# The first token of three short LSTMs in seven block products instead of eight, with the schedule around it retimed

## The chip, the core and the metric

The kernel runs on one core of one Trainium2 chip, and the time is the device time of one execution in microseconds (us). Kernels are timed against each other on the same chip; the number given for a kernel is the median of its runs. One execution is recorded by the profiler; its "span" is the time from its first to its last recorded instruction, a little less than its device time. The names used below: TensorE (PE in the profile; PEld is its weight load), Vector (DVE), Scalar (ACT), GpSimd (POOL) and Sync (SP, which issues the DMAs).

## The reference, cut to what matters

The input x is 128 x 64 x 256 in float32 (batch, tokens, channels), and four layers are added to it in turn. The change lies almost wholly in the second.

```python
def layer(x, L):            # used four times
    return x + L(relu(layernorm(x)))

# layer 0: x normalised adjacency product, linear, batchnorm, relu, linear, batchnorm
# layer 1:
h = relu(einsum('ts,bsh->bth', adj, x @ Wg0 + bg0))
h = relu(einsum('ts,bsh->bth', adj, h @ Wg1 + bg1))
for p in range(1, 5):
    nw = 64 // p                                   # windows of p tokens
    wins = h[:, :nw * p, :].reshape(128 * nw, p, 256)
    last = lstm(Wih[p - 1], Whh[p - 1], bias[p - 1], wins)   # state after p steps, from zero
    h = h.at[:, arange(nw) * p + (p - 1), :].set(last)       # takes the last token's place
return h
# layer 2: attention with one head, a causal mask and an added mask, two linear maps
# layer 3: attention with four heads and a mask from adj
```

A step of an LSTM forms four gates of 256 channels, i, f, g and o, from the token and the state before; then c = sigmoid(f) c + sigmoid(i) tanh(g) and h = sigmoid(o) tanh(c). On the first step state and cell are zero, so the gate f and the products with Whh fall away: three gates, from the token alone.

## The kernel before, in words

**Tiles.** 512 columns (8 batch rows of 64 tokens) are a chunk, and there are 16 chunks. In layer 1 the channels lie on the 128 partitions in two blocks, and two chunks make a pass: a tile `hT` of 128 x 2 x 1024, eight passes in all (`sc` 0 to 7). The LSTM with p = 1 works on 1024 columns, p = 2 on 512, p = 3 on 336 and p = 4 on 256.

**Seven products.** A linear map of 256 channels to 256, with the columns cut in halves, is a 2 x 2 block product. In the usual way it takes eight products of a 128 x 128 weight block with half the columns. The kernel makes most of them in seven, after Strassen and Winograd: sums and differences of the weight blocks are made once at the start (`weight_sums`, L754 to L760, put to DRAM and read back for each p by `load_sets`, L887, as the tile `wset`), those of the operands are made as they are needed (`differences`, L313 to L316: four operations; for tokens of the input on GpSimd into the tile `xd`, for states on Vector into `hd`), and the blocks of the result are added up from the products (L1164, Vector, out of PSUM, after a copy of the first part by Scalar, L1161). The products are numbered 1 to 7: 1 takes the first channel block of the first half of the columns, 2 and 3 take the second channel block of the two halves, 5, 6, 7 and 4 take the differences. Every matmul is in float32, and a product is two matmul instructions in the profile.

**An LSTM with p > 1** (`lstm`, a generator; the numbers at its `yield`s are used below). The first token is done in the usual way: twelve products (three gates, two output blocks, two channel blocks; L1126) over all the columns, into six banks of PSUM of their own (two each of the tags `y`, `z` and `x`). Scalar makes the gates out of PSUM (L1113), Vector the cell (L1119), Scalar its tanh (L1120), Vector the state (`new_state`: L1093 inside a window, L1095 and L1099 for the last step, which goes back into `hT`) and then the differences of the state. The later steps are `Unit`s, one for each gate and step: seven kinds of product, each with a token's part and a state's part (L1155), copies (L1161), adds (L1164), gates (L1084), a GpSimd product of two gates (L1221), the cell (L1234, L1235) and its tanh (L1236). Products of the next step's token are put ahead of the state's: they need no state. The stage for p = 1 (`single`, L1340 to L1364) has seven products for each gate already. While an LSTM ends it has the operands of the next one's second token made (`ending`).

**Order.** The whole stage is written out by hand: on each engine, instructions run in the order in which the program emits them. An LSTM that stops at a `yield` lets other work in: `n` counts the `yield`s (those that yield "a" count a half), and tables say at which numbers the other generators take their next step. `single` has the places 0 to 3, p = 2 has 4 to 7, p = 3 has 8 to 13 and p = 4 has 14 to 21. The other work is: the graph convolutions of chunks of the next pass (`CONV`, `FIRST`, `BEGUN`: norm statistics, `apply`, the aggregations `agg_b` and `agg_c` of 64 short matmuls, and the 16-instruction products `v` (L915, L921) and `u` (L929, L935)); the residual of the pass before (`RESIDUAL`: transposes L1277, a way through DRAM, two adds L284 of 0.68 us); and the norm of layer 2 for chunks that are done (`AHEAD`, `LATE`, `FINAL`: through DRAM, statistics L159 and L160 on Vector, a power on GpSimd, the shift on Vector (L194), four applies on Scalar (L196), transposes). The last pass has no convolutions left; there `IDLE` puts transposes of no use on TensorE.

The middle of the function, with the first token:

```python
products = [(q, c, k) for k in range(KD) for q in GATES[:3] for c in range(KD)]
for at, (q, c, k) in enumerate(products):
    if at == 6:
        yield
    nc.tensor.matmul(banks[q, c][:, :n]..., wsets[p, q][:, 2 * k + c, :], hv[:, k, tokens 0], ...)
first_acts(0, 2); first_cell(0); first_acts(3); first_cell(1)
for c in range(KD):
    new_state(0, c, every)
```

Of the kernel before, what the change touches and what calls it, by code (L numbers as in the profile page):

```python
# [8 lines left out]
F32 = mybir.dt.float32  # L9
AF = mybir.ActivationFunctionType  # L10
# [9 lines left out]
def kernel(  # L20
# [168 lines left out]

    def apply_halves(dst, src, stats, name):  # L190

        mv, rstd = stats
        nmr = small.tile([P, NJ], F32, tag=f"ln_nmr{NJ}", name=f"nmr_{name}")
        nc.vector.scalar_tensor_tensor(nmr, mv[:, :, 0], -1.0, rstd, op0=OP.mult, op1=OP.mult)  # L194
        for j in range(NJ):
            nc.scalar.activation(dst[:, j, :], src[:, j, :], AF.Relu, bias=nmr[:, j : j + 1],  # L196
                                 scale=rstd[:, j : j + 1])
            if j % 2:
                yield
# [487 lines left out]
    with tc.manual_schedule(engines={mybir.EngineType.PE}):  # L687
# [56 lines left out]
        def weight_sums(p, q):  # L744
            w = stage.tile([P, 16, P], F32, tag="ws", name=f"ws_{p}_{q}", bufs=2)
            for i, src in enumerate((wih_t, whh_t)):
                nc.sync.dma_start(
                    w[:, 8 * i : 8 * i + 4, :].rearrange("p (k c) f -> p k (c f)", k=KD),
                    src[p - 1].rearrange("(k p) f -> p k f", p=P)[:, :, q * D : (q + 1) * D])
            yield  # L750
            v = w.rearrange("p (i b) f -> p i b f", i=2)
            for dst, a, b, op in ((4, 1, 3, OP.add), (5, 4, 0, OP.subtract), (6, 0, 1, OP.subtract),
                                  (7, 2, 5, OP.subtract)):
                nc.gpsimd.tensor_tensor(v[:, :, dst], v[:, :, a], v[:, :, b], op)  # L754
            far = dram.tile([P, 15, P], F32, tag=f"ws{p}{q}", name=f"wfar_{p}_{q}", bufs=1)
            nc.sync.dma_start(far[:, :9], w[:, :9])
            nc.sync.dma_start(far[:, 9:], w[:, 10:])
            wfar[p, q] = far
            yield
# [123 lines left out]
    def load_sets(n):  # L883
        for _ in range(min(n, len(coming))):
            p, q = coming.pop(0)
            wsets[p, q] = w1.tile([P, 15, P], F32, tag="wset", name=f"wset_{p}_{q}", bufs=6)
            nc.sync.dma_start(wsets[p, q], wfar[p, q])  # L887
# [92 lines left out]
    def convolutions(c):  # L980
# [18 lines left out]
        stats = ln_stats(xs[c], f"b{c}")  # L999
        yield  # L1000
# [23 lines left out]
    BLOCKS = {1: (0, 8), 2: (2, 9), 3: (7, 14), 4: (3, 10), 5: (4, 11), 6: (5, 12), 7: (6, 13)}  # L1024
# [14 lines left out]
    def operands_x(p, hv, name, s):  # L1039

        nw, nb, inner, tokens = columns_x(p, hv)
        m = nw * nb // 2
        t = l1.tile([P, 7 * (T // 3) * NB], F32, tag="xd", name=f"xd_{name}_{s}", bufs=2)
        t = [t[:, i * m : (i + 1) * m].rearrange("p (a b) -> p a b", b=inner) for i in range(4)]
        b = {(k, j): tokens(k, s, j) for k in range(KD) for j in range(2)}
        for f in differences(nc.gpsimd, t, b[0, 0], b[0, 1], b[1, 0], b[1, 1]):
            f()
        return {5: t[0], 6: t[1], 7: t[2], 4: t[3], 1: b[0, 0], 2: b[1, 0], 3: b[1, 1]}

    def lstm(p, hv, name, follows, x1, ending):  # L1050
# [24 lines left out]
        gates = l1.tile([P, 4, KD, CH], F32, tag="gates", name=f"gates_{name}", bufs=1)  # L1075
        cells = l1.tile([P, KD, CH], F32, tag="cell", name=f"cell_{name}", bufs=1)
        hn = l1.tile([P, KD, CH], F32, tag="hs", name=f"hs_{name}", bufs=1)
        hd = l1.tile([P, 4, CH // 2], F32, tag="hd", name=f"hd_{name}", bufs=1)
# [11 lines left out]
        def new_state(s, c, part, engine=nc.vector):  # L1090
# [6 lines left out]
            else:  # L1097
# [8 lines left out]
        ox = {1: x1}  # L1106

        banks = {(q, c): bank(f"g{q}_{name}_{c}", tag) for q, tag in ((0, "y"), (2, "z"), (3, "x"))
                 for c in range(KD)}
        def first_acts(*qs):  # L1110
            for q in qs:
                for c in range(KD):
                    nc.scalar.activation(  # L1113
                        columns_of(gate(q, c)),
                        natural(banks[q, c][:, :n].rearrange("p (w b) -> p w b", b=nb)),
                        AF.Tanh if q == 2 else AF.Sigmoid, bias=bs[:, q * KD + c : q * KD + c + 1])

        def first_cell(c):
            nc.vector.tensor_mul(cells[:, c, :n], gate(0, c), gate(2, c))  # L1119
            nc.scalar.activation(gate(2, c), cells[:, c, :n], AF.Tanh)  # L1120

        products = [(q, c, k) for k in range(KD) for q in GATES[:3] for c in range(KD)]
        for at, (q, c, k) in enumerate(products):
            if at == 6:
                yield
            nc.tensor.matmul(  # L1126
                banks[q, c][:, :n].rearrange("p (w b) -> p w b", b=nb), wsets[p, q][:, 2 * k + c, :],
                hv[:, k, : (nw - 1) * p + 1 : p, :], start=(k == 0), stop=(k == KD - 1))
        first_acts(0, 2)
        first_cell(0)  # L1130
        first_acts(3)
        first_cell(1)
        for c in range(KD):
            new_state(0, c, every)
            if not c:
                dh[0]()
# [67 lines left out]
        each(A, pe(5, "x"), pe(3, "x"), pe(2, "x"))  # L1204
        yield
        for s in range(1, p):
# [4 lines left out]
            each(A, pe(5, "h"), do("copy", 5), pe(1), do("copy", 1), pe(3, "h"), pe(2, "h"), pe(6), do("u4"),  # L1211
# [88 lines left out]
    def block_sums(b, name):  # L1300

        t = []
        for i in range(2):
            part = l1.tile([P, 7 * (T // 3) * NB], F32, tag="xd", name=f"xd_{name}_{i}", bufs=2)
            for a in range(0, 2 * CH, CH):
                v = part[:, a : a + CH]
# [7 lines left out]
    def single(b, name, t, ending):  # L1314
# [5 lines left out]
        gates = l1.tile([P, 4, KD, CH], F32, tag="gates", name=f"gates_{name}", bufs=1)  # L1320
        cells = l1.tile([P, KD, CH], F32, tag="cell", name=f"cell_{name}", bufs=1)
        more = l1.tile([P, KD, CH], F32, tag="hs", name=f"hs_{name}", bufs=1)
# [90 lines left out]
    operands = {}  # L1413

    def lstms(sc, hT):
# [4 lines left out]
        def ending(p):  # L1420

            if p < SKIP:
                operands[p + 1] = operands_x(p + 1, hv, names[p + 1], 1)
# [40 lines left out]
    def ahead(c):  # L1464

        yield from to_pairs(c)
        stats = ln_stats(xs[c], f"n2_{c}")
        yield
# [16 lines left out]
    RESIDUAL = (0, 3, 4), (2, 5, 5.5)  # L1485
    CONV = (3, 4, 4, 5, 5.5, 7, 8, 9, 10, 10), (3, 4, 4, 11, 11.5, 13, 14, 15, 15.5, 17, 18, 20)
    BEGUN = (11, 11, 13, 14, 16), (17, 17.5, 21)
    FIRST = (1, 2, 3, 3, 4, 4, 5, 5.5, 7, 8, 9, 10, 10), (1, 2, 4, 5, 6, 8, 11, 11.5, 13, 14, 15, 15.5, 17, 18, 20)
    AHEAD = (4, 5, 7, 12, 14, 19), (6, 7)
    LATE = 5, 6, 8, 9  # L1490
    IDLE = {5: 4, 7: 18, 9: 10, 13: 14, 15: 8}
    FINAL = (4, 5, 9.5, 10, 12, 13), (6, 7, 11.5, 14, 14, 15)
# [25 lines left out]
    with tc.manual_schedule(engines={mybir.EngineType.PE, mybir.EngineType.DVE, mybir.EngineType.Pool,  # L1518
                                     mybir.EngineType.Activation, mybir.EngineType.SP}):
        last = NCH // SUP - 1  # L1520
        for sc in range(last + 1):
# [7 lines left out]
            if sc > 1:  # L1529
                units(LATE[:1], aheads[sc * SUP - 3])  # L1530
# [9 lines left out]
            if sc > 1:  # L1540
                units(LATE[1:], aheads[sc * SUP - 3])
# [548 lines left out]
```

## Time and profile before

| | us |
|---|---|
| median of 7 runs | 1868.53 |
| fastest and slowest of them | 1867.3, 1869.97 |
| the profiled execution | 1869.97 |
| its span | 1868.2 |
| first-token products L1126 in it, the first and the last start | 294.3, 1456.2 |
| first-token products L1126 in it, 576 instructions | 185.8 |
| later products L1155 in it, the largest group (1152 instructions) | 255.7 |
| residual adds L284 from `hT`, 32 | 0.68 each |

The profile gives busy time of each engine, a timeline of instructions (start, duration, line, operation, output tile <- input tiles, shape, count, and in brackets how long the engine was idle before it and what ended that), groups of like instructions (count, busy time, mean in ns, idle time before them), the chain of work that ended last in order of time, and the waits of an engine by what it waited for. Matmuls overlap a little in the records, so the busy time of a group is larger than the time that it takes of TensorE; the steps of the chain do not overlap.

### The profile page before, as it was taken

The numbers are of one execution on the slowest core, as the hardware profiler recorded it, in microseconds if no ns is written. First come the engines' busy times: TensorE is split into PE (matmuls) and PEld (weight loads), VectorE is DVE, ScalarE is ACT, GpSimd is POOL, SyncE is SP. The second block draws the span as 40 slices with busy tenths as digits, with TensorE's granted clock in tenths as the row PEclk, the third lists the DMA queues.
The fourth block names the chain that finished last, engine by engine and source line by source line (L and its number), as shares of the span: only waits on it lengthen the run. The fifth ranks groups of instructions, "written<-read, shape, count | busy, mean of one in ns | idle before, by whom it ended". The sixth has DMA issues, their size and how long they took to land.

```text
span 1868.2 us, 39078 instructions
## 1 busy us (share of the span) xinstructions
PE 1846.0 (99%) x15077; PEld 1477.1 (79%) x15077; DVE 1250.8 (67%) x3150; ACT 1013.4 (54%) x2284; POOL 554.0 (30%) x704
## 2 busy tenths in 40 slices
PE   8999989999999999999999999999999999999998
PEld 6877855996897799699589689878969967777776
DVE  5767856567467666667766766766566567776776
ACT  5766635556456455655654655655565534444453
POOL 5865712123122222212322311222132114322232
PEclk9999999999999999999999999999999999999999
DMA  3223651235333533333433443343144244544433
GB/s 115 69 65 140 236 207 57 96 123 169 111 119 141 164 131 131 109 114 121 160 119 120 164 146 126 142 125 124 61 142 149 71 158 136 151 145 144 141 114 114
DMA packets 111273, 241.45 MB, mean 129 GB/s; under 512 B 11504, under 2 KB 74864, under 8 KB 111088
## 3 DMA queue, kind: packets, MB, share of 16 engines
q1 hardware_dynamic: 110192, 237.09, 37.8%
q8 instruction: 119, 1.95, 0.4%
q0 software_dynamic: 320, 1.05, 0.2%
q10 hardware_dynamic: 576, 0.82, 0.1%
q14 instruction: 66, 0.54, 0.1%
HBM read 170.50 MB, written 68.42 MB: 128 GB/s over the span
## 4 chain that ended last, share of the span: by engine, by line
PE 90%; DVE 5%; ACT 2%; issue 1%; POOL 1%; DMA 1%; SPq 0%; DVEq 0%; ACTq 0%; POOLq 0%
PE x L1155 22%; PE z L1155 11%; PE g L1126 9%; PE y L1155 6%; PE v L1580 5%; PE x L1340 4%; PE y L1340 3%; PE u L929 3%; PE v L915 3%; PE p_q L1587 3%; PE X L1776 3%; PE X L423 2%; PE X L499 2%; PE Y L423 1%; PE Y L1776 1%
## 5 line engine op out<-in xcount | busy, mean ns | idle before, releaser
L1155 PE MATMUL x<-xd,wset 128*128 128x128 f32 (+2 forms) x1152 | 255.7, 304 | 1.4 <-DVE gates L1164 1.4
L1155 PE MATMUL x<-hd,wset 128*128 128x128 f32 (+2 forms) x1152 | 254.7, 303 | 0.0
L1221 POOL TENSOR_TENSOR gates<-gates 128x512 f32<-128x512 f32 (+2 forms) x48 | 75.1, 1565 | 498.7 <-ACT gates L1084 498.7
L1164 DVE TENSOR_TENSOR gates<-gates,x 128x128 f32<-128x128 f32 (+2 forms) x384 | 120.7, 320 | 151.3 <-PE x L1155 148.3
L1084 ACT ACTIVATE gates<-gates,bias 128x256 f32<-128x256 f32 (+4 forms) x384 | 172.6, 489 | 90.3 <-DVE gates L1164 90.3
L1164 DVE TENSOR_TENSOR gates<-gates,z 128x128 f32<-128x128 f32 (+2 forms) x384 | 102.2, 317 | 146.3 <-PE z L1155 146.3
L1155 PEld LDWEIGHTS x<-xd,wset 128*128 128x128 f32 x1152 | 187.8, 191 | 7.5 <-DVE gates L1164 2.5
L1155 PEld LDWEIGHTS x<-hd,wset 128*128 128x128 f32 x1152 | 187.8, 191 | 4.9
L1126 PE MATMUL g<-hT,wset 128*128 128x256 f32 (+2 forms) x576 | 185.8, 477 | 0.1
L1126 PEld LDWEIGHTS g<-hT,wset 128*128 128x128 f32 x576 | 109.4, 191 | 69.1 <-issue 39.1
L1161 ACT COPY gates<-y 128x128 f32<-128x128 f32 (+2 forms) x192 | 54.0, 292 | 198.0 <-PE y L1155 196.0
L1155 PE MATMUL z<-hs,wset 128*128 128x128 f32 (+2 forms) x768 | 146.6, 303 | 0.2 <-DVE hs L1093 0.2
L1155 PE MATMUL z<-hT,wset 128*128 128x128 f32 (+2 forms) x768 | 146.5, 303 | 0.0
L1155 PEld LDWEIGHTS z<-hs,wset 128*128 128x128 f32 x768 | 117.2, 191 | 3.9 <-DVE hs L1093 0.6
L1155 PEld LDWEIGHTS z<-hT,wset 128*128 128x128 f32 x768 | 117.2, 191 | 3.4
L1113 ACT ACTIVATE gates<-g,bias 128x512 f32<-128x512 f32 (+2 forms) x144 | 75.2, 559 | 42.3 <-PE g L1126 41.7
L1084 ACT ACTIVATE gates<-x,bias 128x128 f32<-128x128 f32 (+2 forms) x192 | 74.8, 390 | 29.7 <-PE x L1155 26.5
L1155 PE MATMUL x<-hT,wset 128*128 128x128 f32 (+2 forms) x384 | 86.0, 306 | 0.0
L1155 PE MATMUL x<-hs,wset 128*128 128x128 f32 (+2 forms) x384 | 84.9, 303 | 0.0
L1236 ACT ACTIVATE gates<-cell 128x256 f32<-128x256 f32 (+2 forms) x144 | 55.2, 383 | 47.3 <-DVE cell L1235 47.3
L1155 PE MATMUL y<-hd,wset 128*128 128x128 f32 (+2 forms) x384 | 79.4, 309 | 0.0
L1595 POOL TENSOR_TENSOR s<-s,mx 128x256 f32<-128x256 f32 (+2 forms) x33 | 40.4, 1225 | 128.0 <-DVE mx L1594 120.2
(326 smaller groups left out, 4169.5 us busy)
## 6 DMA issues: line engine op xcount, KB each, us to landing
wset<-wfar SPq DMA_DIRECT2D x96, 960.0 KB, 6.6
hT<-far_h SPq DMA_DIRECT2D x124, 128.0 KB, 3.2
far_h<-hm SPq DMA_DIRECT2D x16, 512.0 KB, 2.8
far_n<-xs SPq DMA_DIRECT2D x16, 512.0 KB, 3.4
xs<-far_n SPq DMA_DIRECT2D x64, 128.0 KB, 4.6
far_x<-xs SPq DMA_DIRECT2D x16, 512.0 KB, 3.0
x<-far_x SPq DMA_DIRECT2D x64, 128.0 KB, 3.2
xt<-in_x_dram SPq DMA_DIRECT2D x15, 512.0 KB, 4.1
```

What stands on the lines that cost most here:

```text
L423: nc.tensor.matmul(self.banks[tag][:, i * CH // 2 : (i + 1) * CH // 2], w, self.at[kind], start=first and not i, stop=True, skip_group_che ...
L915: nc.tensor.matmul(banks[m], wg0_sb[:, k, m * P : (m + 1) * P], agg[:, k, :], start=(k == 0), stop=(k == KD - 1))
L929: nc.tensor.matmul(banks[j // 2][:, j % 2, :], v[:, k, j * P : (j + 1) * P], wg1_sb[:, k, :], start=(k == 0), stop=(k == KD - 1))
L1084: nc.scalar.activation(gate(q, c, part), src, AF.Tanh if q == 2 else AF.Sigmoid, bias=bs[:, q * KD + c : q * KD + c + 1])
L1113: nc.scalar.activation(columns_of(gate(q, c)), natural(banks[q, c][:, :n].rearrange("p (w b) -> p w b", b=nb)), AF.Tanh if q == 2 else AF. ...
L1126: nc.tensor.matmul(banks[q, c][:, :n].rearrange("p (w b) -> p w b", b=nb), wsets[p, q][:, 2 * k + c, :], hv[:, k, : (nw - 1) * p + 1 : p, ...
L1155: nc.tensor.matmul(folded(self.psum(kind)), wsets[p, self.q][:, BLOCKS[kind][i], :], (ox[self.s] if part == "x" else oh)[kind], start=firs ...
L1164: nc.vector.tensor_add(gate(self.q, *dst), gate(self.q, *a), self.psum(kind))
L1221: nc.gpsimd.tensor_mul(gates[:, 0, :, :n], gates[:, 0, :, :n], gates[:, 2, :, :n])
L1340: nc.tensor.matmul(folded(ps(g, kind)), wih1[:, g, KINDS1[kind], :], right[kind], start=kind in (2, 5, 1), stop=True, skip_group_check=True)
L1580: nc.tensor.matmul(ps[:, i, :], hT[:, k, j, :], w[:, k, first : first + D], start=(k == 0), stop=(k == KD - 1))
L1776: nc.tensor.matmul(st[c, tag][:, i * CH // 2 : (i + 1) * CH // 2].rearrange("p (a n) -> p a n", n=P), w, st[c, "o7"][kind], start=first an ...
```

## The change

Five things are changed together.

1. The first token of p = 2, 3 and 4 is done in seven products for each gate, by a new class `First`: 21 products of half the columns (L1127 after the change), Scalar's copies of two of them (L1131), Vector's adds (L1134: twelve), gates by `act` (L1095) out of the sums, and for one quarter out of PSUM. The gates 0 and 2 use one bank each of the tags `y` and `z`, gate 3 two of the tag `x`; so the products 1, 6, 7 and 4 of a gate follow each other in one bank. There is one more `yield`, of "a", after the first half of the state. The later products, adds and gates are L1180, L1189 and L1095 there, the cells L1152, L1159, L1259 and L1260, the states L1104, L1106 and L1110, the differences L327 to L330.
2. The plain weight blocks that only the twelve products used leave the sets, which have 14 blocks in place of 15 and are put to DRAM by three DMAs in place of two. The differences of the first token are made on GpSimd like the second's, and the tile `xd` has three buffers in place of two. Of the second token's products ahead of the state, number 5 is moved to its place beside the state's part.
3. The tiles `gates`, `cell`, `hs` and `hd` are made once for the stage in place of once for each LSTM.
4. The statistics of a norm are done in two steps of two tiles each, and the shift (minus mean over deviation) by two operations on GpSimd in place of one on Vector.
5. The tables are new. `agg_b` of the next pass's first chunk, which stood between the twelve products of p = 2, is at place 3, ahead of them; the residual add of the second chunk is at 8.5 in place of 5.5; the norm of layer 2 begins in one pass and ends in the next for both chunks.

```diff
+    def norm_halves(src, name):
...
+        for j in range(NJ):
+            nc.vector.bn_stats(st[:, j, :], src[:, j, :])
+            nc.vector.bn_aggr(mv[:, j, :], st[:, j, :])
+            if j == NJ // 2 - 1:
+                yield
...
+        rsqrt(rstd, mv[:, :, 1], EPS)
+        nc.gpsimd.tensor_tensor(nmr, mv[:, :, 0], rstd, OP.mult)
+        nc.gpsimd.tensor_scalar(nmr, nmr, -1.0, None, op0=OP.mult)
+        yield rstd, nmr
...
-            wsets[p, q] = w1.tile([P, 15, P], F32, tag="wset", name=f"wset_{p}_{q}", bufs=6)
+            wsets[p, q] = w1.tile([P, 14, P], F32, tag="wset", name=f"wset_{p}_{q}", bufs=6)
...
-        t = l1.tile([P, 7 * (T // 3) * NB], F32, tag="xd", name=f"xd_{name}_{s}", bufs=2)
+        t = l1.tile([P, 2 * CH], F32, tag="xd", name=f"xd_{name}_{s}", bufs=3)
...
-        gates = l1.tile([P, 4, KD, CH], F32, tag="gates", name=f"gates_{name}", bufs=1)
-        cells = l1.tile([P, KD, CH], F32, tag="cell", name=f"cell_{name}", bufs=1)
-        hn = l1.tile([P, KD, CH], F32, tag="hs", name=f"hs_{name}", bufs=1)
-        hd = l1.tile([P, 4, CH // 2], F32, tag="hd", name=f"hd_{name}", bufs=1)
+        gates, cells, hn, hd = lstm_tiles
...
+        class First:
+
+            def __init__(self, q, tags):
+                self.q, self.ps = q, [bank(f"{t}{q}_{name}_{i}", t) for i, t in enumerate(tags)]
+
+            def psum(self, kind):
+                return self.ps[kind in (5, 3)][:, m:n] if kind in (2, 3) else self.ps[kind in (5, 3)][:, :m]
+
+            def product(self, kind):
+                nc.tensor.matmul(folded(self.psum(kind)), wsets[p, self.q][:, BLOCKS[kind][0], :], ox[0][kind],
+                                 start=kind in (1, 5), stop=True, skip_group_check=True)
...
+        firsts = [First(q, tags) for q, tags in ((0, "yz"), (2, "yz"), (3, "xx"))]
+
+        def all_first(*fs):
+            for f in fs:
+                for u in firsts:
+                    f(u)
...
+        all_first(made(1), lambda u: u.copy(0, 0, 1), made(5), lambda u: u.copy(1, 1, 5))
+        yield
+        all_first(made(2), lambda u: u.add((0, 0), (0, 0), 2), made(3), made(6), lambda u: u.add((0, 1), (1, 1), 6),
+                  made(7), lambda u: u.add((1, 1), (1, 1), 7), lambda u: u.add((0, 1), (0, 1), 3), made(4),
+                  lambda u: act(u.q, 0, every, gate(u.q, 0)))
+        nc.vector.tensor_mul(cells[:, 0, :n], gate(0, 0), gate(2, 0))
+        nc.scalar.activation(gate(2, 0), cells[:, 0, :n], AF.Tanh)
+        all_first(lambda u: act(u.q, 1, halves[0], u.psum(4)),
+                  lambda u: act(u.q, 1, halves[1], gate(u.q, 1, halves[1])))
+        new_state(0, 0, every)
+        dh[0]()
+        yield "a"
...
-        each(A, pe(5, "x"), pe(3, "x"), pe(2, "x"))
+        each(A, pe(3, "x"), pe(2, "x"))
...
-            each(A, pe(5, "h"), do("copy", 5), pe(1), do("copy", 1), pe(3, "h"), pe(2, "h"), pe(6), do("u4"),
+            each(A, pe(5, "h" if s > 1 else "xh"), do("copy", 5), pe(1), do("copy", 1), pe(3, "h"), pe(2, "h"), pe(6), do("u4"),
...
-                operands[p + 1] = operands_x(p + 1, hv, names[p + 1], 1)
+                operands[p + 1] = {s: operands_x(p + 1, hv, names[p + 1], s) for s in range(2)}
...
-    RESIDUAL = (0, 3, 4), (2, 5, 5.5)
-    CONV = (3, 4, 4, 5, 5.5, 7, 8, 9, 10, 10), (3, 4, 4, 11, 11.5, 13, 14, 15, 15.5, 17, 18, 20)
-    BEGUN = (11, 11, 13, 14, 16), (17, 17.5, 21)
-    FIRST = (1, 2, 3, 3, 4, 4, 5, 5.5, 7, 8, 9, 10, 10), (1, 2, 4, 5, 6, 8, 11, 11.5, 13, 14, 15, 15.5, 17, 18, 20)
-    AHEAD = (4, 5, 7, 12, 14, 19), (6, 7)
-    LATE = 5, 6, 8, 9
+    RESIDUAL = (0, 3, 5.5), (2, 5, 8.5)
+    CONV = (3, 4, 5, 5.5, 7, 8, 9, 10, 10), (5, 5, 6, 9.5, 11, 11.5, 13, 14, 15, 15.5, 17, 18, 20)
+    BEGUN = (11, 11, 14.5, 17, 17, 20, 21), (17.5, 19, 21)
+    FIRST = (1, 1, 1, 2, 3, 4, 4, 5, 5.5, 7, 8, 9, 10, 10), (1, 2, 4.5, 5, 5, 6, 9.5, 11, 11.5, 13, 14, 15, 15.5, 17, 18, 20)
+    AHEAD = (6, 7), (9, 10)
+    LATE = (4.5, 4.5, 5.5, 9, 19.5), (9, 9.5, 11, 12, 21)
+    LATEST = (4.5, 4.5, 5.5, 9, 9.5), (9.5, 9.5, 10, 11, 11.5)
     IDLE = {5: 4, 7: 18, 9: 10, 13: 14, 15: 8}
-    FINAL = (4, 5, 9.5, 10, 12, 13), (6, 7, 11.5, 14, 14, 15)
+    FINAL = (6, 7, 11, 11, 12, 15, 15.5), (9, 10, 13, 13, 16, 17, 17.5)
...
-            if sc > 1:
-                units(LATE[:1], aheads[sc * SUP - 3])
...
             if sc > 1:
-                units(LATE[1:], aheads[sc * SUP - 3])
+                for i in range(SUP):
+                    units((LATEST if sc == last else LATE)[i], aheads[(sc - 2) * SUP + i])
```

## The prediction, made before the changed kernel was run

> **What bounds the kernel now.** I read the page's first part, then the busy time by stage, then what TensorE waited for while the LSTMs run, then the timeline around the places that the diff touches.
>
> ```profile
> span 1868.2 us, 39078 instructions
> ...
> PE 1846.0 (99%) x15077; PEld 1477.1 (79%) x15077; DVE 1250.8 (67%) x3150; ACT 1013.4 (54%) x2284; POOL 554.0 (30%) x704
> ```
>
> Busy time by stage; this is one pass over two chunks in the LSTM stage (TensorE, weight loads, Vector, Scalar, GpSimd, granted clock, DMA):
>
> ```profile
> 580.00:726.00 146.00, 145.77 (x1027) 118.42 (x1026) 97.54 (x257) 82.21 (x197) 37.06 (x44) 1.00 0.38 132
> ```
>
> TensorE's waits between 290 and 1470 us are only these:
>
> ```profile
> PE x L1155 <- DVE gates L1164: 1.4, 6, 0.2
> PE agg_b L214 <- ACT cv L196: 1.2, 1, 1.2
> PE y L1155 <- ACT gates L1113: 0.7, 1, 0.7
> ```
>
> So TensorE is the limit: 3.3 us of waiting in 1180, at full clock. Products taken away are time saved, one for one; every wait that the change brings is time lost, one for one.
>
> **The products: 20.0 us saved.** The chain in order of time has the first tokens of p = 3 and p = 4, and fillers of known size:
>
> ```profile
> 490.91 3.45 PE u L929 x16
> 494.37 6.78 PE g L1126 x24
> 502.86 1.09 PE agg_c L214 x64
> ...
> 539.08 5.18 PE g L1126 x24
> 545.60 3.46 PE u L929 x16
> ```
>
> A product is two instructions. 24 instructions of 336 columns take 6.78 us, of 256 columns 5.18; of 512 columns twice 5.15 (605.23, x12). Together 22.26 a pass. After, each has 21 products of half the width. One of 256 columns is 3.46/8 = 0.4325 us, one of 168 is 0.285 (steps 506.83, 507.12, 507.40), one of 128 is 0.2235 (551.12 to 551.34). 21 x (0.4325 + 0.285 + 0.2235) = 9.08 + 5.99 + 4.69 = 19.76. Saved 2.50 a pass, 20.0 over eight.
>
> **The waits inside the 21 products.** The old order ran twelve products into six banks with no reader between. The new one reuses a bank: 7 needs Vector's add of 6, 4 needs the add of 7, and only two other products stand between. The turnaround:
>
> ```profile
> 507.12 0.45 PE L1155 MATMUL x<-hd,wset 128*128 128x168 f32 x2
> 507.40 0.45 PE L1155 MATMUL x<-xd,wset 128*128 128x168 f32 x2
> 507.67 0.33 DVE L1164 TENSOR_TENSOR gates<-gates,x 128x168 f32<-128x168 f32 x1 [3.49 <-PE x L1155]
> ```
>
> The product's slot ends at 507.40, the add starts 0.27 later and takes 0.33; Vector to TensorE is 0.05 (an add of 560.57 ends, the product starts at 560.90). p = 3: 0.65 against two slots of 0.57, twice 0.07, 0.15 in all. p = 4: 0.27 + 0.28 + 0.05 = 0.60 against 0.447, twice, 0.31. p = 2: 0.74 against 0.865, nothing. Eight passes: 2.5 us for p = 4; p = 3's 0.15 is in the next part.
>
> **The wait for token 0's state, p = 3.** Before, Scalar's gates began when 7 of 12 products were done. Now every gate waits for adds at the end, and the products that need the state come after four x products and the filler. Counted from the first of the 21: the sixes' first ends at 3.71, the products at 6.13; Vector's last-but-three adds end at 5.80 and the first add of 3 at 6.05 (0.33 alone, 0.245 back to back: two took 0.57 at 531.19). Then Scalar:
>
> ```profile
> L1084 ACT ACTIVATE gates<-gates,bias 128x336 f32<-128x336 f32 x64 | 34.8, 570 | 24.5 <-DVE gates L1164 24.5
> ```
>
> 0.57, 0.46 for each one behind it: two done at 7.10; cell product 0.51, 7.65; tanh 0.48, 8.15; state 0.51 and its difference 0.33, 9.05. TensorE stands at 6.13 + 1.14 (four x) + 1.09 (agg) + 0.285 = 8.65 and gets the operand at 9.10: 0.45 lost. For the second channel block Scalar does three gates from PSUM (0.40, then 0.30) and two of 0.42 and 0.33 by 9.75, but Vector's queue has two residual adds between (moved to 8.5 of the schedule; L284 from hT, 20.5 us for 32, 1.28 a pair): 10.35. Product, tanh, state (0.51 + 0.48 + 0.51): 11.93. TensorE has seven more products of cover, until 11.10: 0.83 lost. Last, two chunk applies of 0.54 stand on Scalar ahead of the copies that free the banks for 6: about 0.2. Sum 0.15 + 0.45 + 0.83 + 0.2 = 1.65 in passes 2 to 7; pass 1 has no apply (1.43), pass 0 no residual add either (1.0). Total 12.3 us. At p = 4 the filler is u (3.46): operand at 7.6, wanted at 9.4. At p = 2 it is v (3.43): 12.7 against 14.7, the second block 17.0 against 17.7 with four statistics of 0.53 in Vector's queue. No cost there; without that cover it would be 1 to 2 us each.
>
> **The start of p = 2.** Products 1 and 5 use channel block 0, product 2 the last state of the single-step stage:
>
> ```profile
> 605.07 4.46 PE L1126 MATMUL g<-hT,wset 128*128 128x512 f32 x10
> ...
> 607.95 1.20 DVE L1356 TENSOR_TENSOR hT<-cell,gates 128x512 f32<-128x512 f32 x1 [0.16 <-ACT gates L1353]
> ```
>
> It lands at 609.15, 4.1 us after that stage's last product. Before, 5.15 us of products and agg_b covered it. After, agg_b (1.1, moved ahead) and six products (2.6) give 3.7: 0.44 lost with the hand-over, in six passes, 2.6 us. In passes 3 to 6 four transposes (1.42 at 1418.99), placed at 21, go ahead of the single stage's adds. Part of the delay is absorbed; I take 0.55 each, 2.2 us, between 0 and 1.4.
>
> **The last pass** has no convolutions, only idle transposes whose number is unchanged:
>
> ```profile
> 1372.29 10.46 PE L1126 MATMUL g<-hT,wset 128*128 128x512 f32 x24
> ...
> 1376.03 1.19 DVE L1356 TENSOR_TENSOR hT<-cell,gates 128x512 f32<-128x512 f32 x1 [0.17 <-ACT gates L1353]
> ```
>
> The state lands 4.9 us after 1372.3, cover is 2.6: 2.3 lost. At p = 2 the state of token 0 then comes 1.05 and 1.2 late (0.45 of filler in place of 3.43). At p = 3 the state lands 2.66 after the first product, against 1.71: 0.95. At p = 4, 0.74, and the statistics of chunk 13 (2.1 us) stand ahead of the first adds, 1.0 more; then 0.6 and 0.4 as above with 0.9 of filler. Sum 8.2, of which 0.7 was there before (the third wait above): 7.5.
>
> **Parts that I cost at nothing.** The weight set is one block of fifteen smaller (960 KB, 6.6 us to land, no TensorE wait on a DMA in the stage); the far copy takes three issues in place of two, twelve more on SP while Seven2 runs, where SP is ahead. If it were not, one landing of 2.8 us each way bounds it. Norm shifts: Vector loses an operation of about 0.15 us, GpSimd gains 0.20 + 0.24 (L356, L357) behind a power of 1.04. The reader is Scalar's apply, and of TensorE's waits only agg_b's 1.2 us comes from an apply: between -0.3 and +0.4 us a chunk, 0 taken. One tile for the stage drops waits like Scalar's at 590.81 on GpSimd's state; TensorE waited for none of them, 0, at best -0.8 a pass. Block operands of token 0: four more GpSimd operations, 24 times (0.54 at 168); in p = 3 done 2.4 us after the start, wanted at 3.4; late by the whole 1 us only if GpSimd is held by other work.
>
> A row on that: the state of 607.95 took 1.20 us beside GpSimd's L315, the same line 0.69 at 607.09. The Trainium skill, page "SBUF — State Buffer", section "SBUF: two separate sides", says that Vector with two SBUF inputs and GpSimd take one shared port by an exclusive lock for a whole instruction. By that rule the new block adds (one input in PSUM) would be untouched and the sum stands as it is; if every start lost the 0.5 us of that row, it would be 24 x 0.5 = 12 us worse.
>
> **Sum.** -20.0 + 2.5 + 12.3 + 2.6 + 2.2 + 7.5 = +7.1 us. The profiled execution took 1869.97 us (span 1868.2 and 1.8 around it), 1.4 over the median of 1868.53. So 1877 for it, **1875.5** for the median; I say 1875. Each wait is a difference of long chains, good to perhaps 0.3 us, and the same one repeats in seven or eight passes.
>
> **Rivals.** (1) **Token 0's state is back in time.** One place: p = 3, Scalar's gates. It decides if the operand is there 8.65 us after the first product instead of 9.10, and the second by 11.1 instead of 11.9, as when Scalar's gates go out faster than 0.46 apiece or the residual add slips into a gap. Then the 12.3 shrinks to 0.15 x 8 = 1.2 and the last pass, having the same chain, to about half, 3.7: -20.0 + 2.5 + 1.2 + 2.6 + 2.2 + 3.7 = -7.8, 1860.5. For it: Vector is 67% and Scalar 54% busy. Against: they are idle because they wait in this very chain. (2) **Waits and saving cancel**, the sum lying 4 to 10 us lower than mine: 1868.5. For it: all the waits are computed, none seen. (3) **Queues run into each other**: Vector gets 12 more adds a start and the waits above feed the next ones, with 0.5 us (1.20 against 0.69 at 607) for each of 24 starts: +7.1 + 12 = 1887.5. Against: three adds take 0.82 us at p = 3 and three products 0.855. (4) That the change does not do what it says: the instruction order of the changed kernel shows 21 half products at each of 24 starts, so no chance of its own.
>
> **How the numbers follow.** Forecast 0.46, rival 1 0.27, rival 2 0.19, rival 3 0.08. A measurement tells 0.2% (3.7 us) from no change: faster 0.27, same 0.19, slower 0.54. From 1858 to 1885: from rival 1's time less 2.5 (the bounds of the small parts) to most of the way to rival 3; its far end and a full saving are left out. The forecast's own range is 1872 to 1883.
>
> **What would show it.** L1126 is replaced by L1127 with 504 products, TensorE busy down by about 20 us, idle up by 27. Waits of L1180 on hd and hs (L327, L1104) near 0.45 and 0.8 at each p = 3, waits of L1127 on Vector near 0.15 at p = 4, waits of L1127 on hT (L1378) of 0.4 and, in the last pass, above 2. If p = 3's waits are absent, rival 1 holds. I would be wrong by more if TensorE's busy time did not fall by 20 us, or waits came on GpSimd's xd.

## The result, and the profile after

The changed kernel takes **1873.48 us** (median of 13 runs, 1872.77 to 1874.33), the kernel before 1868.04 on the same chip (33 runs, 1867.3 to 1869.97). The ratio is 1.0028 with a 95% interval of 1.0021 to 1.0036: 5.4 us slower, where 7 were forecast.

The first part of the page, after:

```profile
span 1870.9 us, 40786 instructions
...
PE 1838.8 (98%) x15509; PEld 1513.5 (81%) x15509; DVE 1321.7 (71%) x3410; ACT 1051.3 (56%) x2500; POOL 613.4 (33%) x856
```

TensorE's busy time fell by 7.2 us, not by 20. That isn't a smaller saving: the records of a product's two matmuls run 0.45 us where its slot (the time from its start to the next one's in an unbroken row) is 0.285, so a wait of up to 0.16 us shows as busy time. The waits that are long enough to show, between 285 and 1470 us (waited-for line: total, times, longest):

```profile
PE z L1180 <- DVE l_hs L1104: 3.7, 8, 0.8
PE x L1362 <- DVE l_gates L1386: 2.3, 1, 2.3
PE y L1127 <- DVE hT L1378: 2.2, 7, 1.1
PE x L1127 <- ACT l_gates L1367: 1.0, 1, 1.0
PE y L1127 <- ACT l_gates L1131: 0.9, 2, 0.6
PE y L1127 <- POOL xd L328: 0.7, 1, 0.7
PE y L1180 <- ACT l_gates L1095: 0.6, 1, 0.6
```

They add up to 11.4 us (two more, of 0.3 and 0.2, are left out here), where before there were 3.3. To see the short ones too, take the time from the start of each matmul to the start of the next, less the usual slot of its shape: in the LSTM stage that excess is about 35 us before (some 20 of it at the short agg matmuls) and about 58 after, 23 more, against 20 saved. The table below says the same: its three longest stretches (pass 0, passes 1 to 6, last pass) are 3.1 us longer in all, with 20.0 us of products less. The lengths of the stretches, from the starts of their first matmuls; the third column belongs to the first experiment, the last pass is taken to the first matmul of layer 2:

| us | before | after | twelve_all |
|---|---|---|---|
| pass 0 | 158.92 | 158.02 | 156.90 |
| pass 3, p = 1 and p = 2 | 60.68 | 60.17 | 60.96 |
| pass 3, p = 3 | 44.71 | 45.19 | 44.71 |
| pass 3, p = 4 | 48.12 | 47.61 | 47.56 |
| passes 1 to 6 | 920.74 | 917.52 | 919.09 |
| last pass | 143.16 | 150.38 | 142.05 |

So the loss is not spread: seven passes are 4.1 us shorter, the last is 7.2 longer. The rest of the program differs by less than 1 us on either side. (The two profiled executions, 1869.97 and 1872.77 us, are the slowest of the first and the fastest of the second, so the traces can place 2.8 of the 5.4 us.)

### The profile page after: what moved, and what is told of

It reads as the page before. It is cut to its first block, busy times and chain, and to the rows that moved or that the text cites. A ratio compares the mean times of both kernels' runs of the same rounds, so it can differ in the third digit from the quotient of the medians.

```text
span 1870.9 us, 40786 instructions
## 1 busy us (share of the span) xinstructions
PE 1838.8 (98%) x15509; PEld 1513.5 (81%) x15509; DVE 1321.7 (71%) x3410; ACT 1051.3 (56%) x2500; POOL 613.4 (33%) x856
## 4 chain that ended last, share of the span: by engine, by line
PE 83%; DVE 9%; ACT 4%; POOL 2%; issue 1%; DMA 1%; SPq 0%; DVEq 0%; ACTq 0%; POOLq 0%
PE x L1180 22%; PE z L1180 11%; PE y L1180 5%; PE v L1605 5%; PE y L1127 4%; PE u L943 3%; PE v L929 3%; PE p_q L1612 3%; PE y L1362 3%; PE X L1801 3%; PE x L1362 3%; PE x L1127 2%; PE X L437 2%; PE X L513 2%; PE z L1127 1%
## 5 line engine op out<-in xcount | busy, mean ns | idle before, releaser
L1095 ACT ACTIVATE l_gates<-l_gates,bias 128x256 f32<-128x256 f32 (+4 forms) x528 | 238.1, 498 | 211.9 <-DVE l_gates L1189 110.0
L1180 PE MATMUL x<-xd,wset 128*128 128x128 f32 (+2 forms) x1152 | 255.1, 303 | 0.2 <-ACT l_gates L1186 0.2
L1180 PE MATMUL x<-l_hd,wset 128*128 128x128 f32 (+2 forms) x1152 | 254.6, 303 | 0.0
L1189 DVE TENSOR_TENSOR l_gates<-l_gates,z 128x128 f32<-128x128 f32 (+2 forms) x384 | 102.3, 317 | 130.6 <-PE z L1180 128.6
L1180 PEld LDWEIGHTS x<-xd,wset 128*128 128x128 f32 x1152 | 187.8, 191 | 5.8 <-issue 0.5
L1180 PEld LDWEIGHTS x<-l_hd,wset 128*128 128x128 f32 x1152 | 187.9, 191 | 4.9
L1189 DVE TENSOR_TENSOR l_gates<-l_gates,x 128x128 f32<-128x128 f32 (+2 forms) x384 | 121.1, 321 | 92.2 <-PE x L1180 88.4
L1180 PE MATMUL z<-l_hs,wset 128*128 128x128 f32 (+2 forms) x768 | 147.3, 304 | 3.7 <-DVE l_hs L1104 3.7
L1180 PE MATMUL z<-hT,wset 128*128 128x128 f32 (+2 forms) x768 | 146.2, 303 | 0.0
L1180 PEld LDWEIGHTS z<-l_hs,wset 128*128 128x128 f32 x768 | 116.8, 191 | 9.4 <-DVE l_hs L1104 6.1
L1180 PEld LDWEIGHTS z<-hT,wset 128*128 128x128 f32 x768 | 117.2, 191 | 3.3
L1095 ACT ACTIVATE l_gates<-x,bias 128x128 f32<-128x128 f32 (+2 forms) x216 | 84.7, 392 | 30.8 <-PE x L1180 28.1
L1180 PE MATMUL x<-hT,wset 128*128 128x128 f32 (+2 forms) x384 | 85.9, 305 | 0.0
L1180 PE MATMUL x<-l_hs,wset 128*128 128x128 f32 (+2 forms) x384 | 84.9, 303 | 0.0
L327 POOL TENSOR_TENSOR xd<-hT 128x128 f32<-128x128 f32 (+2 forms) x72 | 42.5, 590 | 128.2 <-DVE hT L1106 100.0
L1180 PE MATMUL y<-l_hd,wset 128*128 128x128 f32 (+2 forms) x384 | 83.6, 310 | 0.3 <-DVE l_hd L327 0.2
L1180 PE MATMUL y<-xd,wset 128*128 128x128 f32 (+2 forms) x384 | 81.9, 305 | 0.9 <-ACT l_gates L1095 0.6
```

The costliest lines, as they stand in the source:

```text
L1095: nc.scalar.activation(gate(q, c, part), src, AF.Tanh if q == 2 else AF.Sigmoid, bias=bs[:, q * KD + c : q * KD + c + 1])
L1180: nc.tensor.matmul(folded(self.psum(kind)), wsets[p, self.q][:, BLOCKS[kind][i], :], (ox[self.s] if part == "x" else oh)[kind], start=firs ...
L1189: nc.vector.tensor_add(gate(self.q, *dst), gate(self.q, *a), self.psum(kind))
```

## The experiments

**1. Twelve products again, the rest as changed** (`twelve_all`). The old block with its yield "a" after the first half of the state, sets of 15 blocks, two `xd` buffers, and no differences of the first token on GpSimd.

```diff
-        all_first(made(1), lambda u: u.copy(0, 0, 1), made(5), lambda u: u.copy(1, 1, 5))
...
+        products = [(q, c, k) for k in range(KD) for q in GATES[:3] for c in range(KD)]
+        for at, (q, c, k) in enumerate(products):
...
```

> The changed kernel with the first token of every LSTM back in twelve full products (15-block weight sets and two xd buffers, as before the change, since both do not fit beside each other); its tables, the norm's two halves, the shifts on GpSimd and the single set of tiles stay. Theory 1 (all of the +5.4 us is the seven products' own balance: 20.0 us of TensorE saved, 23 us of new waits in the LSTM stage): 1868 to 1870, waits of the stage back near 36 us by the starts of the matmuls, of which agg steps are some 20. Theory 2 (the products gain, and the retimed tables and moved norm operations cost more than that): clearly above 1873.5, up to 1890 if the whole 20 us were won net.

Measured 1865.84 (0.9988, 0.9979 to 0.9997): a little faster than before. TensorE waits in the stage, between 290 and 1470 us:

```profile
PE x L1401 <- DVE l_gates L1425: 2.3, 1, 2.3
PE z L1219 <- DVE l_hs L1108: 0.2, 1, 0.2
```

Theory 1 holds in its cause, but the time lies 2.2 us below its range: seven products cost 7.6 us against this kernel, and the other parts of the change win 2.4 against the kernel before. (The wait of 2.3 us stands in both lists, so it is not the seven products'.) Against it, the seven products change passes 0 to 6 by -0.45 us in all (saving and waits cancel almost exactly) and the last pass by +8.3.

**2. Twelve products in the last pass alone** (`twelve_last`).

```diff
+        if old_first(p, name):      # sc == 7
+            products = [(q, c, k) for k in range(KD) for q in GATES[:3] for c in range(KD)]
...
+        else:
             all_first(made(1), lambda u: u.copy(0, 0, 1), made(5), lambda u: u.copy(1, 1, 5))
```

> The changed kernel with twelve full products in the last pass alone, seven in passes 0 to 6. Theory 1 (the last pass, without convolutions to lie between, lost 7.2 us from its start to the start of layer 2, and passes 0 to 6 won 4.1): the last pass falls from 150.4 to about 143 to 145 us, total 1866 to 1868, below the kernel before. Theory 2 (the last pass loses by its new tables, not by the seven products): the last pass stays at 148 to 150 us, total 1872 to 1873.5.

Measured 1869.34 (1.0003, 0.9994 to 1.0012). The last pass fell to 142.05, so its loss is the seven products', not the new tables'. But the total stayed above theory 1's 1866 to 1868: p = 3 had grown from 45.19 to 45.82 us in passes 1 to 6. The kernel differs there only in the weight sets and in two `xd` buffers for three, which the next one separates.

**3. Two xd buffers, nothing else** (`xd_two_buffers`).

```diff
-        t = l1.tile([P, 2 * CH], F32, tag="xd", name=f"xd_{name}_{s}", bufs=3)
+        t = l1.tile([P, 2 * CH], F32, tag="xd", name=f"xd_{name}_{s}", bufs=2)
```

> The changed kernel with two xd buffers in place of three, nothing else. Theory 1 (what kept twelve_last at 1869.3 in place of 1866 is the missing third buffer: GpSimd waits 1.49 us for the old one and then runs beside Vector's cell and state of p = 3, which take 0.80 and 0.83 us in place of 0.51): p = 3 grows from 45.19 to 45.8 us in passes 1 to 6, total 1877 to 1878. Rival (it was the 15-block set): 1873.5.

The tile is made at two places, and both have the edit. Measured 1879.0 (1.0059, 1.0045 to 1.0073), p = 3 at 45.81: the buffer. The time lies 1 us above theory 1's range; the last pass grew too, by 0.8 us. In p = 3 of pass 3, first GpSimd, then Vector:

```profile
807.00 0.54 POOL L327 TENSOR_TENSOR xd<-hT 128x168 f32<-128x168 f32 x1 [1.49 <-PE x L1127]
807.50 0.54 POOL L328 TENSOR_TENSOR xd<-hT 128x168 f32<-128x168 f32 x1
807.99 0.81 POOL L329 TENSOR_TENSOR xd<-hT,xd 128x168 f32<-128x168 f32 x1
```

```profile
807.59 0.81 DVE L1152 TENSOR_TENSOR l_cell<-l_gates 128x336 f32<-128x336 f32 x1 [0.63 <-ACT l_gates L1095]
808.95 0.83 DVE L1104 TENSOR_TENSOR l_hs<-l_gates 128x336 f32<-128x336 f32 x1 [0.55 <-ACT l_gates L1153]
```

The late GpSimd operations are not waited for. They harm by running beside Vector's cell and state, which then take 0.81 and 0.83 us in place of 0.51, in the chain that TensorE waits for: 0.62 us together, as much as p = 3 grew.

**4. The residual add of the second chunk half a place later** (`residual_9`).

```diff
-    RESIDUAL = (0, 3, 5.5), (2, 5, 8.5)
+    RESIDUAL = (0, 3, 5.5), (2, 5, 9)
```

> The changed kernel with the residual add of the second chunk at place 9 in place of 8.5, so behind the second half of p = 3's first state on Vector. Theory 1 (the two adds of 1.28 us stand ahead of the second cell product, which waits for Scalar's gates only until 0.5 us earlier): the wait of z on the state in p = 3, 0.59 us net in passes 1 to 6, falls to about 0.1, total -3 us, 1870.5. Rival (Scalar's order, six gates and a tanh, holds the second half anyway): wait unchanged, 1873.5.

Measured 1873.46 (1.0026, 1.0016 to 1.0036). Neither theory as written: the wait on the state went in passes 1 to 6, and no time was won. In p = 3 of pass 3, Vector and then TensorE:

```profile
809.74 1.28 DVE L298 TENSOR_TENSOR xs<-xs,hT 128x512 f32<-128x512 f32 x2
...
812.03 0.55 DVE L1189 TENSOR_TENSOR l_gates<-l_gates,x 128x168 f32<-128x168 f32 x2
```

```profile
808.90 1.41 PE L1180 MATMUL z<-l_hs,wset 128*128 128x168 f32 x8
...
812.39 0.55 PE L1180 MATMUL x<-xd,wset 128*128 128x168 f32 x2 [0.37 <-DVE l_gates L1189]
```

The two adds now stand, with two statistics behind them, ahead of the block adds of the next step, and TensorE waits there: p = 3 takes 45.36 us in passes 2 to 6, where it took 45.19. From 808.34 to 813 Vector has no gap in this trace; a move inside such a stretch only names another wait. (In pass 1, which has no such statistics, the same move won 0.47 us.)

**5. and 6. The small parts undone** (`undo_small`: the shift on Vector and new tiles for each LSTM; `shift_vector`: the shift alone).

```diff
-        nc.gpsimd.tensor_tensor(nmr, mv[:, :, 0], rstd, OP.mult)
-        nc.gpsimd.tensor_scalar(nmr, nmr, -1.0, None, op0=OP.mult)
+        nc.vector.scalar_tensor_tensor(nmr, mv[:, :, 0], -1.0, rstd, op0=OP.mult, op1=OP.mult)
         yield rstd, nmr
...
-        gates, cells, hn, hd = lstm_tiles
+        gates, cells, hn, hd = new_tiles()      # undo_small alone
```

> The changed kernel with the norm's shift back on Vector in one operation, and the four tiles made anew for each LSTM; seven products, tables and the two halves of the statistics stay. Theory 1 (these parts cost and bring nothing, as the prediction took them): 1873.5, within 1.5. Rival (one of them is part of the loss, or hides a gain): 2 us or more away on either side.

> The changed kernel with only the norm's shift back on Vector; the single set of tiles stays. Theory 1 (in undo_small, 35 us slower, the whole loss is that Scalar's first copy must wait until the last reader of the old tiles is done, Vector's state of the LSTM before; the trace shows that copy idle 1.39 us for it): 1873.5, within 1.5. Rival (the shift in one Vector operation delays applies and with them the chain): between 1880 and 1908.

Measured 1908.65 (1.0213, 1.0199 to 1.0227) and 1904.77 (1.0194, 1.018 to 1.0208). I had put the 35 us down to the tiles; it was the shift, and the tiles are left with 3.9. The second time lies in the rival's range, but no wait of TensorE on an apply came with it; what came was in Vector's queue. Vector in `shift_vector`:

```profile
DVE nmr_n L202 <- POOL rstd_n L100: 21.4, 14, 2.4
DVE nmr_b L202 <- POOL rstd_b L100: 20.5, 14, 1.5
```

An operation of 0.16 us stands directly behind GpSimd's power and holds Vector's whole queue, 41.9 us in 28 waits. TensorE then waits 14.8 us for block adds and 8.5 for states in that trace.

**7. The shift on Vector, one yield later** (`shift_vector_late`), as before the change.

```diff
     def apply_halves(dst, src, stats, name):
+        nc.vector.scalar_tensor_tensor(nmr, mv[:, :, 0], -1.0, rstd, op0=OP.mult, op1=OP.mult)
```

> The changed kernel with the shift back on Vector where it was before the change: with the applies, one yield after the power on GpSimd, not directly behind it as in shift_vector. Theory 1 (the 31 us of shift_vector come from Vector's queue standing 1.3 to 2.4 us for GpSimd's power, 28 times and more, not from the operation): 1873.5 to 1875. Rival (the operation on Vector costs wherever it stands): above 1885.

Measured 1878.37 (1.0052, 1.0037 to 1.0067): 4.9 over the changed kernel, beyond what theory 1 allowed, far below the rival. The place is worth 26 us, the operation itself 5; its trace is 2.1 us longer than the changed kernel's in pass 0, 1.6 in passes 1 to 6 and 1.8 in the last pass. Why the operation costs as much there was not followed further.

**8. New tiles with twelve products** (`twelve_own_tiles`): `twelve_all` with the `new_tiles()` of the diff above.

> Twelve full products everywhere as in twelve_all, and the four tiles made anew for each LSTM. Theory 1 (a new set of tiles costs only where a writer comes early, and with twelve products Scalar's first gate comes seven products after the start): 1866, within 1.5. Rival (the new tiles cost in any case): far above, near 1900.

Measured 1867.08 (0.9992, 0.9982 to 1.0001); every section is as long as in `twelve_all` within 0.15 us. As theory 1 has it: new tiles cost nothing clear here, where the first writer comes late, and about 4 us with `First`, whose copies write them early. (In `undo_small` TensorE waits 6.0 us in 9 places for those copies, in `shift_vector` 0.6 in 2.)

**9. to 12. Seven products where they pay.** `seven_p2_steady` has them for p = 2 in passes 1 to 6 and twelve products elsewhere. The others try to remove its wait at the start of p = 2: `seven_p2_early_hm` moves four transposes, `seven_p2_swap` puts product 3 ahead of 2, `seven_p2_after_state` forms GpSimd's differences in another order.

```diff
+        return int(p > 2 or sc in (0, 7))      # old_first, in all four
...
-    RESIDUAL = (0, 3, 5.5), (2, 5, 8.5)        # seven_p2_early_hm
+    RESIDUAL = (0, 3, 5.5), (1, 5, 8.5)
...
-            all_first(made(2), lambda u: u.add((0, 0), (0, 0), 2), made(3), made(6), ...    # seven_p2_swap
+            all_first(made(3), made(2), lambda u: u.add((0, 0), (0, 0), 2), made(6), ...
...
-        for f in differences(nc.gpsimd, t, b[0, 0], b[0, 1], b[1, 0], b[1, 1]):    # seven_p2_after_state
-            f()
+        if p == 2 and s == 0:
+            t1, t2, t3, t4 = t
+            for dst, x, y, op in ((t1, b[0, 1], b[0, 0], OP.subtract), (t4, b[1, 0], b[1, 1], OP.subtract),
+                                  (t2, b[1, 1], t1, OP.subtract), (t3, b[1, 1], b[0, 1], OP.subtract),
+                                  (t4, t4, t1, OP.add)):
+                nc.gpsimd.tensor_tensor(dst, x, y, op)
+        else:                                  # the four differences as before
...
```

> Seven products only for p = 2 in passes 1 to 6, twelve everywhere else. From the section lengths of the profiles: p = 1 and p = 2 together take 60.67 to 60.97 us a pass with twelve and 59.86 to 60.17 with seven, p = 3 44.71 against 45.19, p = 4 47.56 against 47.60. Theory 1 (the sections add up, each pays by itself): 1865.8 - 6 x 0.8 = 1861, below both kernels. Rival (what p = 2 wins is lost in the next section's waits): 1865 to 1866.

> As seven_p2_steady, with the four transposes of the second chunk's residual (2.1 us on Vector) at place 1 in place of 2, so not directly ahead of the last gates of p = 1. Theory 1 (they make the state late that the first products 2 of p = 2 wait for, 0.43 net a pass): that wait falls to 0 to 0.1, 1858.5. Rival (on Vector they only push the earlier adds of p = 1, and TensorE waits there instead): no gain, 1861, or a loss of up to 1 us a pass.

> As seven_p2_steady, with product 3 ahead of product 2. Product 3 needs the half of the last state of p = 1 that Vector writes first, product 2 the half that it writes last. Theory 1 (the wait at the start of p = 2, 0.43 net a pass, is for that last half alone, and three products of 0.43 more cover it): the wait goes, 1862.2 - 6 x 0.43 = 1859.7. Rival (the adds of 2 then come later and something behind them waits): 1862.

> As seven_p2_steady, with GpSimd's differences for the first token of p = 2 formed in another order, with one operation more (first the difference of the two states of channel block 1, which waits for the last state, then the others), so that GpSimd starts after Vector's last state of p = 1 and not beside it. Theory 1 (that state takes 1.20 us in place of 0.69 because GpSimd works beside it): it takes 0.69, lands 0.5 us earlier, the wait at the start of p = 2 (0.43 net a pass) goes, 1862.2 - 6 x 0.43 = 1859.7. Rival (the 1.20 has another cause, as its layout): it stays 1.20 and the time 1862.2; or the later differences make product 6 wait: above 1862.2.

| kernel | us | ratio to before, interval | p = 2, pass 3 |
|---|---|---|---|
| seven_p2_steady | 1862.24 | 0.9964, 0.9952 to 0.9977 | 40.66 |
| seven_p2_early_hm | 1869.44 | 1.0004, 0.9995 to 1.0013 | 40.96 |
| seven_p2_swap | 1865.02 | 0.9983, 0.9974 to 0.9992 | 41.11 |
| seven_p2_after_state | 1859.18 | 0.9952, 0.9938 to 0.9965 | 40.28 |

The first is nearest to theory 1 (1861): the sections add up, to 1 us. The second is its rival, and worse: p = 1 grew from 19.52 to 20.81 us, because TensorE now waits for block adds behind the moved transposes. The third is a miss of both: product 3, which goes into the same bank as product 5, had to wait for Scalar's copies of 5, and these for the last state of p = 1, which still reads the part of `l_gates` that they write:

```profile
PE z L1131 <- ACT l_gates L1135: 3.3, 6, 0.6
```

The same state was waited for, by another way. The fourth is theory 1. GpSimd and Vector in `seven_p2_steady`:

```profile
757.42 0.73 POOL L328 TENSOR_TENSOR xd<-hT 128x256 f32<-128x256 f32 x1 [2.69 <-DVE hT L1417]
758.11 1.18 POOL L329 TENSOR_TENSOR xd<-hT,xd 128x256 f32<-128x256 f32 x1
```

```profile
757.51 1.20 DVE L1417 TENSOR_TENSOR hT<-l_cell,l_gates 128x512 f32<-128x512 f32 x1 [0.17 <-ACT l_gates L1414]
```

and in `seven_p2_after_state`:

```profile
756.55 0.74 POOL L1069 TENSOR_TENSOR xd<-hT 128x256 f32<-128x256 f32 x1 [3.55 <-DVE hT L1424]
```

```profile
755.77 0.69 DVE L1424 TENSOR_TENSOR hT<-l_cell,l_gates 128x512 f32<-128x512 f32 x1 [0.17 <-ACT l_gates L1421]
```

With one GpSimd operation more, but none beside it, the state takes 0.69 us and the wait is gone. This kernel is 9 us faster than before and 14 faster than the change.

## Why the prediction was right

**The sign and the size held, and so did the main reason**: 20 us of products saved, a little more than that in new waits. Term by term, against the kernel before unless said otherwise:

- **The saving.** In p = 3 of pass 3 the 21 products take 6.36 us with 0.37 of waiting, 5.99 without: as computed.
- **Inside the 21 products, p = 4: 0.31 forecast, 0.53 measured.** The turn between two trios was sized well: the first product of the next trio comes 0.17 and 0.19 late, near the 0.15 of the sum. What the sum left out is that a product behind a wait takes longer itself, here by 0.10 and 0.07 us (its two matmuls start 0.21 and 0.19 us apart in place of 0.11, at 845.89 and 846.85). The row before the change from which the hand-over was read has it too: 0.49 us for the two matmuls at 560.90, in place of 0.39. At p = 3 the same turns 0.15 into 0.37 (0.09 and 0.11 late, 0.10 and 0.08 longer). Against `twelve_all`, p = 4 wins nothing (47.61 and 47.56).
- **p = 3: 1.65 forecast, 1.28 measured** (net of what was there). This is the chain that carried the forecast; Scalar, Vector and TensorE after the change, from the first of the 21 at 797.18:

```profile
803.31 1.50 ACT L1095 ACTIVATE l_gates<-l_gates,bias 128x336 f32<-128x336 f32 x3 [3.92 <-DVE l_gates L1134]
```

```profile
804.38 0.51 DVE L1152 TENSOR_TENSOR l_cell<-l_gates 128x336 f32<-128x336 f32 x1 [0.63 <-ACT l_gates L1095]
805.44 0.51 DVE L1104 TENSOR_TENSOR l_hs<-l_gates 128x336 f32<-128x336 f32 x1 [0.55 <-ACT l_gates L1153]
805.98 0.33 DVE L327 TENSOR_TENSOR l_hd<-l_hs 128x168 f32<-128x168 f32 x1
806.23 1.28 DVE L298 TENSOR_TENSOR xs<-xs,hT 128x512 f32<-128x512 f32 x2
807.44 0.50 DVE L1159 TENSOR_TENSOR l_cell<-l_gates 128x336 f32<-128x336 f32 x1
808.48 0.51 DVE L1104 TENSOR_TENSOR l_hs<-l_gates 128x336 f32<-128x336 f32 x1 [0.55 <-ACT l_gates L1160]
```

```profile
806.37 0.55 PE L1180 MATMUL y<-l_hd,wset 128*128 128x168 f32 x2
...
809.05 1.41 PE L1180 MATMUL z<-l_hs,wset 128*128 128x168 f32 x8 [0.42 <-DVE l_hs L1104]
```

The gates start at 6.13 (forecast 6.05 plus the hand-over), the difference is done at 9.13 (9.05), the second state at 11.81 (11.93). The chain was right within about 0.1 us; TensorE stood elsewhere. It lost 0.37 inside the 21 products (forecast 0.15), so it came later to the operand and waited 0.21 there (0.45) and 0.59 at the second block (0.83). The applies cost nothing (0.2).
- **The start of p = 2: 0.44 forecast, 0.43 measured**; ahead of it, behind the transposes in passes 3 to 6, 0.29 in place of the 0.55 that was taken between 0 and 1.4.
- **The last pass**, all terms together: -2.50 + 0.31 + 1.65 + 7.5 = +7.0 forecast, +7.2 measured. The start of its p = 2:

```profile
1369.24 0.70 PE L1127 MATMUL x<-hT,wset 128*128 128x256 f32 x2 [0.97 <-ACT l_gates L1367]
...
1372.32 1.10 PE L1127 MATMUL y<-hT,wset 128*128 128x256 f32 x4 [1.09 <-DVE hT L1378]
```

The first of these waits was not foreseen: product 1 of the third gate takes a bank that Scalar still reads for its last gate of p = 1; with twelve products, four of twice the columns came ahead of that gate. It cost nothing on top, since the state lands 4.94 us after the first product (forecast 4.9) in any case, and both waits together are 2.5 us (2.3). By section the agreement is less good, and partly luck: p = 2, 3 and 4 were to lose 3.3, 1.8 and 1.9 us net of their saving, and lost 3.6, 2.4 and 1.3. At p = 4 two of the waits, 0.7 and 0.3 us, were for GpSimd's `xd`, which the prediction had named as a sign against it.
- **Parts costed at nothing.** Together they cost nothing: with twelve products the kernel with them is 2.4 us faster than before. But "nothing" hid what they are for: without the third buffer the changed kernel is 5.5 us slower, with the shift on Vector 4.9, with its own tiles about 4 (the difference of two kernels that both have the shift on Vector). The first and the third carry the seven products; the second, put between -0.3 and +0.4 a chunk and taken as 0, is 4.9 us over 28 norms, 0.18 each in the mean: inside the bounds, but it adds up.

The forecast was 4 us too dark in passes 0 to 6 (+0.1 against -4.1 in the traces), about half of it at p = 3, the rest at p = 1 and in the gain of the other parts at p = 4; since the traces hold 2.8 of the 5.4 us, up to 2.6 of the 4 may lie in which executions were recorded. One sign failed for a reason that is not the change's: TensorE's busy time did not fall by 20 us, because short waits count as busy. Rival 1 fell: the state is not back in time at p = 3 in any of passes 1 to 6. Rival 2, a cancelling, is what passes 0 to 6 do by themselves against `twelve_all`. Rival 3 was not seen: the adds keep pace at p = 2 and, but for the 0.37 us, at p = 3. At p = 3 it was close: GpSimd's last operation ends at 804.40, 0.02 us into Vector's cell of 804.38; with two `xd` buffers it comes later, and the price is the 0.62 us of experiment 3.

Left open: where `twelve_all` wins its 2.4 us over before. In the traces its last pass is 1.1, its pass 0 2.0 and its passes 1 to 6 together 1.7 us shorter (more than the medians give, since the recorded execution of before is its slowest), but none of its parts was put into the kernel before alone.

## What to carry to other kernels

Fewer products on the busiest engine are worth their time only where other work lies between a result and its next use, so price them place by place: here p = 2 in the steady passes wins 0.8 us, p = 3 loses 0.5, p = 4 wins nothing, and the last pass, with nothing to put between, loses more than the rest wins. When a wait comes back under another name as soon as its cause is moved inside a queue (experiments 4 and 10), look whether that queue has any gap left there; another order in it won nothing here. What did win was to take the work away that ran beside a late operation and slowed it (experiment 12). A short operation that reads another engine's long one is priced by what stands behind it in its own queue: one of 0.16 us cost 31 in one place and 5 in another.

## What the runs showed of the hardware

A Vector operation with both inputs in SBUF was held where it started behind a GpSimd operation that was still at work, and GpSimd's in turn where it started second: 0.51 became 0.81 and 0.83, 0.69 became 1.20, and GpSimd's 0.74 became 1.18; with GpSimd's operations behind it, the state was back at 0.69. In `xd_two_buffers` all 16 Vector operations of 128x336 that started 0.07 to 0.10 us behind a GpSimd one took 0.80 to 0.83; the 64 with none beside them took 0.51. Vector's block adds, with one input in PSUM, ran at 0.28 us each beside the same GpSimd operations:

```profile
799.57 0.56 DVE L1134 TENSOR_TENSOR l_gates<-l_gates,y 128x168 f32<-128x168 f32 x2
```

```profile
799.65 0.54 POOL L330 TENSOR_TENSOR xd<-hT,xd 128x168 f32<-128x168 f32 x1
```

Over the LSTM stage of the changed kernel, a record of such an add of 128x168 has a median of 0.33 us both for the 121 that started while GpSimd was in a `tensor_tensor` of 0.4 us or more and for the 215 that ran with none.

The Trainium skill, page "SBUF — State Buffer", section "SBUF: two separate sides", states that when Vector has two inputs in SBUF and GpSimd reads SBUF, whichever starts first holds a shared port pair for its whole instruction and the other waits. This case agrees: the operations with two SBUF inputs were held, the adds with one were not. The turns fit too: in `seven_p2_steady` the state that starts at 757.51 ends at 758.71, 0.56 us after the GpSimd operation that was at work when it started (757.42 to 758.15), where alone it takes 0.69; the next GpSimd operation starts at 758.11 and takes 1.18. The prediction's row is the same case before the change: the state of 607.95 started behind GpSimd's L314 (607.86, 0.73 us), and L315 (608.55, 1.18 us), which the prediction names, started second.

A wait of TensorE under 0.16 us is in its busy time: the listed waits grew by 8.6 us, the excess by the starts of the matmuls by 23. A product behind a wait takes 0.07 to 0.10 us longer itself.
